# Graph layer with edge softmax: the sums of the weights in wider matmuls as a step of their own, and a new order of steps and gathers

## Chip, cores and metric

The kernel runs on one core of a Trainium2 chip. Its time is the device time of one execution in microseconds (us); lower is better. Before the change the median of 14 runs is 2747.45 us (2735.13 to 2751.48). Engine names: PE is TensorE (PEld its loading of weights), DVE is VectorE, ACT is ScalarE, POOL is GpSimd, SP is SyncE, which here issues the DMAs of loads and stores.

## The reference

There are 6250 nodes with 512 features and 100000 edges, sorted by destination. Two residual layers follow each other. The first one is graph attention with 8 heads of 64 features, the second one averages over neighbours.

```python
h = jnp.maximum(_layernorm(x), 0.0)
# first layer
h = leaky_relu(h @ W.T + b, 0.2).reshape(N, 8, 64)
e_src = sum(h * w_att_src, -1); e_dst = sum(h * w_att_dst, -1)
e = leaky_relu(e_src[src] + e_dst[dst], 0.2)
ex = exp(e - segment_max(e, dst)[dst])
s = segment_sum(ex, dst)
a = ex / s[dst] * edge_attr
x = x + segment_sum(h[src] * a[:, :, None], dst).reshape(N, 512)
# second layer: layernorm and relu again, then mean over the incoming
# edges, two matmuls, bias, layernorm with gamma and beta, residual
```

## The kernel before

**Stages.** A prologue computes `h` and the two attention terms and writes them to DRAM as a table with rows of 520 numbers (512 features and 8 source terms). Then comes the first edge layer, which is where the change lies; by the trace it runs from about 296 to 1440 us. The second edge layer and a tail end the program.

**Tiling of the first edge layer.** The edges, sorted by destination, are cut into four streams q = 0 to 3, worked side by side, as two pairs p = 0, 1 of two streams q2 = 0, 1 each. A window k (NW = 66 of them) takes T = 3 tiles j of 128 edges from each stream; the last window has one tile. The edges of a window of one stream fall on at most 64 destination nodes, so a one-hot matrix of 128 edges by 64 nodes (`oh`) adds a tile up by a matmul. The two streams of a pair fill the two halves of the 128 output partitions. Whatever belongs to a node that goes on in the next window is carried over by one more matmul with a selection matrix.

**Steps of a window.** A hand-written list, ORDER, is walked once per round k from -4 to 66. Each name in it is a step; STEPS gives it an offset, so that a round works on several windows at once (software pipelining). The instructions go to the engines' queues in this order, and each engine runs its own queue in order. The steps that the text speaks of, with line and engine:

- FT0, FT1 (L781, PE) transpose the one-hot matrices of a later window; FT0c, FT1c (L785, ACT) copy them out; FD (L793, PE) fetches destination terms; ECa, ECb (L810, ACT) pick the source terms out of the gathered rows; SSa, SSb (L802, PE) add them, transposed; EZ (L816, ACT) copies the logits.
- SCF (L822), NX (L829), SCR (L836), on DVE, are scans that find each segment's maximum; TE and TM (L848, PE) transpose logits and maxima back; CM (L853, ACT) copies them; LM (L860, DVE) is the leaky relu, SUB (L864, DVE) subtracts the maximum, EXP (L870, ACT) is the exponential `ex`, and AA (L878, L882, DVE) multiplies it by the edge attribute to the weight `aa`.
- D0a, D0b (p = 0, j = 0 and 1) and D1a, D1b (p = 1) multiply gathered rows by their weights on DVE (L942, both streams at once). The third tile is shared: D0c (L949, DVE) takes half of a stream, H01 to H03 and H10 to H13 (L961, ACT, four instructions each) take the rest.
- Apj (add_up, PE) adds tile j of pair p. L974 holds two matmuls (one for each stream) of 64 columns of weights and 512 moving columns. L977 holds two more with the same weights and 9 moving columns of `ex` (8 heads and a column of ones): the sums of the weights. C0, C1 (finish, PE) add the carry, L985 for the features and L986 for the sums. EV0, EV1 (evac, ACT) copy the results out of PSUM, L995 for the features and L997 for the sums; EV1 also issues the stores of the window. A float32 matmul leaves two matmul records and two weight-load records in the trace.
- OH (L762) and CS (L773), on DVE, build the one-hot and the carry selection. AT0, AT1 turn the edge attributes every tenth window. FL, FDf, FX, RS, RH, PF, F9a, F9b and RESC (offset windows below KR = 9 only) handle corrections of the first windows.
- S is a place for one step of "slot" work (L1042 to L1064: final division, residual, layernorm and relu of a finished block of 128 nodes, mostly on DVE), L the last of it. 48 of the 66 rounds have a slot.

**Gathers.** POOL issues one indirect DMA for each stream and tile (L719), twelve in a window, at the end of each round for the window four ahead (NB = 4 buffers). TILES gives their order, as pairs of stream q and tile j. A gather overwrites the rows of the window that has just been worked on, so the one for (q, j) waits for the add-up of tile j of pair q // 2.

**SP** issues, at the head of a round, the loads of edge data and slots, then the stores after EV1, then the store of the slot's relu.

Of the kernel before, what the change touches and what calls it, by code (L numbers as in the profile page):

```python
# [11 lines left out]
AF = mybir.ActivationFunctionType  # L12
# [3 lines left out]
N, D, E, H = 6250, 512, 100000, 8  # L16
# [20 lines left out]
AW = 521  # L37
# [7 lines left out]
def gnn_kernel(ctx, tc, x, srcp, dstp, attrp, wt0, b0, wsrc, wdst, wts, wtn, bias1, gamma1, beta1, out):  # L45
    nc = tc.nc
    V, A, G, S, P = nc.vector, nc.scalar, nc.gpsimd, nc.sync, nc.tensor
# [17 lines left out]
    def bank(tag, bufs=1):  # L65
        if tag == "m":
            m_[0] ^= 1
            tag, bufs = ("b", "f")[m_[0]], 1
        return ps.tile([128, 512], FT, name="ps_" + tag, tag=tag, bufs=bufs)
# [630 lines left out]
    GT, ES_, OHs, OHTs, PEN, AT, ZP, E_, PB, ET, MF, MR, NX, EX, AA, WS, WC, CS, FP, FD, RS, F9, SA, AP_ = ({} for _ in range(24))  # L700
    breg = {}

    def njof(k):
        return T if k < NW - 1 else 1
# [227 lines left out]
    BK, SV, A2 = {}, {}, {}  # L932
# [30 lines left out]
    def add_up(k, p, j):  # L963
        if j >= njof(k):
            return
        oh, ex, g_ = OHs[k], EX[k], GT[k]
        if j == 0:
            BK[p] = bank("w", 2)
            if p == 0:
                SV[k] = bank("sf"[k % 2])[:, 0:32].rearrange("p (a c) -> p a c", a=2)[:, :, 0:H + 1]  # L970
        w, sv = BK[p], SV[k]
        for q2 in range(2):
            r = slice(64 * q2, 64 * q2 + 64)
            P.matmul(w[r, :], oh[:, p, j, q2], g_[:, 2 * p + q2, j, 0:D], start=(j == 0), stop=False, skip_group_check=True)  # L974
        for q2 in range(2):
            r = slice(64 * q2, 64 * q2 + 64)
            P.matmul(sv[r, p], oh[:, p, j, q2], ex[:, j, 2 * p + q2], start=(j == 0 and p == 0), stop=False,  # L977
                     skip_group_check=True)

    def finish(k, p):  # L980

        w, sv = BK.pop(p), SV[k]
        if k:
            c = WC[k] if k < KR else WS[k - 1]
            P.matmul(w, CS[k][:, p], c[:, p, 0:D], start=False, stop=True, skip_group_check=True)  # L985
            P.matmul(sv[:, p], CS[k][:, p], c[:, p, D:AW], start=False, stop=True, skip_group_check=True)  # L986
        BK[k, p] = w
        if p:
            GT.pop(k)

    def evac(k, p):
        w, sv = BK.pop((k, p)), SV[k]
        if p == 0:
            WS[k] = lp.tile([128, 2, AW], FT, name="ws")
        A.activation(WS[k][:, p, 0:D], w, AF.Copy)  # L995
        if p:
            A.activation(WS[k][:, :, D:AW], sv, AF.Copy)  # L997
            for d_ in (OHs, EX, AA, A2, SV, WC, CS):
                d_.pop(k, None)
            WS.pop(k - 2, None)  # L1000
# [71 lines left out]


    TILES = [(int(t[0]), int(t[1])) for t in """
    10 00 11 20 01 21 31 32 30 12 22 02
    """.split()]

    for q in range(NQ):
# [8 lines left out]
    def later(f, end=NW):  # L1087

        return lambda k, *a: f(k, *a) if 0 < k < end else None

    def evac1(k):
        evac(k, 1)
        for p in range(2):
            store(k, p, acc0_d, AW)

    def evac0(k):
        evac(k, 0)
# [3 lines left out]
    def slot(w):  # L1101
# [8 lines left out]
        FT0=(4, front_turn, 0), FT0c=(4, front_copy, 0), FT1=(3, front_turn, 1), FT1c=(3, front_copy, 1),  # L1110
        FD=(3, front_dst), ECa=(3, soft_pick, 0), SSa=(3, soft_src, 0), ECb=(2, soft_pick, 1), SSb=(2, soft_src, 1), EZ=(2, soft_copy), SCF=(2, max_before), NX=(2, max_ahead),
        SCR=(1, max_all), TE=(1, soft_turn, 0), TM=(1, soft_turn, 1), CM=(1, soft_back), LM=(1, leaky),
        SUB=(1, soft_sub), EXP=(1, soft_exp), AA=(1, weigh),
        FL=(1, later(fac_leaky, KR)), FDf=(1, later(fac_sub, KR)), FX=(1, later(fac_exp, KR)), RS=(1, later(fac_rows, KR)),
        RH=(1, later(fac_diag, KR)), PF=(1, later(fac_spread, KR)), F9a=(1, later(fac_rest, KR)), F9b=(1, later(fac_all, KR)),
        RESC=(0, later(rescale, KR)), D0c=(0, message_part), D0a=(0, message, 0, 0), D0b=(0, message, 0, 1), D1a=(0, message, 1, 0),
        D1b=(0, message, 1, 1),
        A00=(0, add_up, 0, 0), A01=(0, add_up, 0, 1), A02=(0, add_up, 0, 2),
        A10=(0, add_up, 1, 0), A11=(0, add_up, 1, 1), A12=(0, add_up, 1, 2), C0=(0, finish, 0), C1=(0, finish, 1),
        EV0=(0, evac0), EV1=(-1, evac1), OH=(4, onehot), CS=(0, later(carry_sel)))  # L1120
    STEPS.update({f"H{p}{i}": (0, message_act, p, i) for p in range(2) for i in range(4) if p or i})
    ORDER = """
    FT1 D1a S S S D0a S D0b H10 A00 CS H11 TE H02 EV1 NX S H01 SCR S D0c A01 RESC TM H03 ECb AT0 FL FT1c SSb OH A10 A02
    S FDf D1b H12 FX RH L CM LM EZ H13 SUB C0 EXP AT0c RS AT1 PF SCF A11 AT1c FT0 S S S F9a A12 FD F9b ECa S SSa S EV0
    FT0c AA S C1
    """.split()

    def late_x(i):
# [6 lines left out]
    for k in range(-4, NW + 1):  # L1135
        sl_ = slot_run(slot(k - 3)) if slot(k - 3) is not None and slot(k - 3) not in LATE else none()
        c, kk = divmod(k, CH)
# [54 lines left out]
    def late_stats(i):  # L1192
        s6 = lp.tile([128, 6], FT, name="s6_0")
        V.bn_stats(s6, keep[:, i])
        V.bn_aggr(lmv[:, i], s6)

    def late_scales(i):
        c, mv = late_part(i), lmv[:, i[0]:i[-1] + 1]
        yield from rstd_of(lp, mv[:, :, 1], LATES, "lt", c[:, :, 9], n=len(i))
        V.scalar_tensor_tensor(c[:, :, 10], mv[:, :, 0], -1.0, c[:, :, 9], op0=OP.mult, op1=OP.mult)  # L1200
# [22 lines left out]
    a = late_scales(one)  # L1223
# [277 lines left out]
    def late_newton(i):  # L1501
        if not 0 <= i < NLATE:
            return
        v = LT[i]
        for _ in v["gen"]:
            yield True
        nb = small.tile([128, 1], FT, name="nb1")
        V.scalar_tensor_tensor(nb, v["mv"][:, 0:1], -1.0, v["rs"], op0=OP.mult, op1=OP.mult)
        v["nb"] = nb
        yield True  # L1510
# [74 lines left out]
    k = NW - 1  # L1585
# [28 lines left out]
    for i in range(-1, NLATE + 4):  # L1614
# [13 lines left out]
        a, b = late_stats(i - 1), late_newton(i - 3)  # L1628
# [9 lines left out]
    with tc.If(fv > 0):  # L1638
# [32 lines left out]
        def logit(ix):  # L1671
            hg = lp.tile([128, RW], FT, name="ghg")
            fetch(hg, h0_d, ix[:, 0:1])
            e = lp.tile([128, H], FT, name="ge")
            fetch(e, ed_d, ix[:, 1:2])
            V.tensor_tensor(out=e, in0=e, in1=hg[:, D:RW], op=OP.add)
            V.scalar_tensor_tensor(e, e, 0.2, e, op0=OP.mult, op1=OP.max)
            return hg, e
# [13 lines left out]
        with tc.For_i(0, NE * 128, 128) as r:  # L1692
            ix, eq = ends(r)
            hg, e = logit(ix)
# [13 lines left out]
        with tc.For_i(0, NE * 128, 128) as r:  # L1708
            ix, eq = ends(r)
            hg, e = logit(ix)  # L1710
# [64 lines left out]
```

## Time and profile before

The profiled execution took 2745.76 us; its span is 2744.0 us, 1.76 us lie around it. It is 1.69 us below the median of the 14 runs.

| stretch, us | length | PE busy | DVE busy | ACT busy | POOL busy | granted PE clock |
|---|---|---|---|---|---|---|
| 0 to 296, prologue | 296 | 213.13 | 214.18 | 138.72 | 174.69 | 0.94, then 0.84 |
| 296 to 440, first edge layer, start | 144 | 116.86 | 90.46 | 77.15 | 85.07 | 0.84 |
| 440 to 1440, first edge layer | 1000 | 825.70 | 676.33 | 594.78 | 637.46 | 0.89 |
| 1440 to 1480, between the layers | 40 | 34.76 | 33.82 | 21.98 | 7.53 | 0.91 |
| 1480 to 2700, second edge layer | 1220 | 985.55 | 559.66 | 267.96 | 793.82 | 0.89 |
| 2700 to 2744, tail | 44 | 20.60 | 30.71 | 11.74 | 17.87 | 0.81 |

| group of instructions, whole span | records | busy us | mean ns |
|---|---|---|---|
| L719 POOL, gathers of the first edge layer | 784 | 765.1 | 976 |
| L974 PE, features added up | 1568 | 503.0 | 699 |
| L961 ACT, steps H | 1788 | 452.0 | 338 |
| L942 DVE, steps D | 260 | 311.5 | 1210 |
| L985 PE, carry of the features | 228 | 143.6 | 709 |
| L977 weight loads | 776 + 792 | 69.1 + 67.4 | 156, 149 |

How to read such lines: a group's line has line number, engine, operation, output and inputs, shapes, count, then busy time and mean duration, and behind the bar the engine's idle time just before these instructions, with what ended it. On a timeline the first number is the start, the second the duration; idle time before the instruction stands in brackets. The ends of matmuls are modelled, so durations of neighbours on PE overlap; the text takes differences between starts. "issue" is a wait for which the profile shows no releaser.

### The profile page before, as it was taken

The numbers are of one execution on the slowest core, as the hardware profiler recorded it, in microseconds if no ns is written. First come the engines' busy times: TensorE is split into PE (matmuls) and PEld (weight loads), VectorE is DVE, ScalarE is ACT, GpSimd is POOL, SyncE is SP. The second block draws the span as 40 slices with busy tenths as digits, with TensorE's granted clock in tenths as the row PEclk, the third lists the DMA queues.
The fourth block names the chain that finished last, engine by engine and source line by source line (L and its number), as shares of the span: only waits on it lengthen the run. The fifth ranks groups of instructions, "written<-read, shape, count | busy, mean of one in ns | idle before, by whom it ended". The sixth has DMA issues, their size and how long they took to land.

```text
span 2744.0 us, 35822 instructions
## 1 busy us (share of the span) xinstructions
PE 2196.6 (80%) x9688; PEld 1090.0 (40%) x9688; DVE 1605.2 (58%) x3323; ACT 1112.3 (41%) x3439; POOL 1716.4 (63%) x1679
## 2 busy tenths in 40 slices
PE   7994488878788888788884488898887879888875
PEld 5762244433333433343432133343443434343433
DVE  8876466566767667676766222354544545454556
ACT  5751355565565656565654111122222222222212
POOL 4665566666666666666652666666666666666662
PEclk9996689899989898888887689898999989998988
DMA  6634576777777878888874767787878777777862
GB/s 204 203 114 134 153 210 195 224 242 231 239 236 240 250 233 242 243 242 240 239 232 140 242 212 237 230 253 249 257 247 263 242 247 246 252 252 249 256 206 90
DMA packets 264718, 611.73 MB, mean 223 GB/s; under 512 B 63604, under 2 KB 74372, under 8 KB 264510
## 3 DMA queue, kind: packets, MB, share of 16 engines
q0 software_dynamic: 125440, 414.35, 50.7%
q1 hardware_dynamic: 138494, 193.97, 21.6%
q8 instruction: 79, 1.29, 0.2%
q14 instruction: 129, 1.06, 0.1%
q10 hardware_dynamic: 576, 1.05, 0.1%
HBM read 511.44 MB, written 97.76 MB: 222 GB/s over the span
## 4 chain that ended last, share of the span: by engine, by line
PE 49%; issue 17%; DVE 12%; POOL 8%; DMA 6%; ACT 4%; another core or an unknown queue 2%; SPq 2%; ACTq 0%; DVEq 0%; POOLq 0%
PE ps_w L974 12%; PE ps_w L1285 7%; POOL g L1249 6%; PE ps_w L985 4%; PE ps_b L573 4%; PE ps_s L1285 3%; PE ps_f L573 3%; PE ps_z L793 3%; DMA gbuf<-h_d,idx 2%; DMA g<-h_d,idx 2%; PE ps_t L781 2%; POOL gbuf L719 2%; PE ps_z L802 1%; DVE gbuf L942 1%
## 5 line engine op out<-in xcount | busy, mean ns | idle before, releaser
L719 POOL DMA_INDIRECT gbuf<-h_d,idx x784 | 765.1, 976 | 439.7 <-issue 188.3
L1249 POOL DMA_INDIRECT g<-h_d,idx x784 | 773.7, 987 | 386.7 <-issue 218.2
L974 PE MATMUL ps_w<-gbuf,oh 128*64 128x512 f32 x1568 | 503.0, 699 | 31.1 <-issue 21.2
L961 ACT ACTIVATE gbuf<-gbuf,aa 128x64 f32<-128x64 f32 x1788 | 452.0, 338 | 2.2 <-DVE aa L882 1.7
L1285 PE MATMUL ps_w<-g,oh 128*64 128x512 f32 x1048 | 332.1, 662 | 108.6 <-issue 56.7
L942 DVE TENSOR_TENSOR gbuf<-gbuf,ps_c 128x1024 f32<-128x1024 f32 x260 | 311.5, 1210 | 0.0
L1285 PE MATMUL ps_s<-g,oh 128*64 128x512 f32 x520 | 159.1, 647 | 31.6 <-issue 29.1
L1285 PEld LDWEIGHTS ps_w<-g,oh 128*64 128x64 f32 x1048 | 75.6, 144 | 258.1 <-issue 241.9
L860 DVE SCALAR_TENSOR_TENSOR et<-ps_b,et 128x192 f32<-128x192 f32 x66 | 23.4, 355 | 259.0 <-issue 203.7
L608 POOL TENSOR_TENSOR pr<-hr,watt 128x1024 f32<-128x1024 f32 x47 | 113.5, 2416 | 90.9 <-DVE hr L606 75.1
L995 ACT ACTIVATE ws<-ps_w 128x512 f32<-128x512 f32 x132 | 78.4, 594 | 198.8 <-PE ps_t L781 32.7
L985 PE MATMUL ps_w<-ws,cs 128*128 128x512 f32 x228 | 143.6, 709 | 11.1 <-issue 10.2
L1367 DVE TENSOR_TENSOR lo<-ps_z,hi 128x512 fp32r<-128x512 f32 x48 | 33.1, 689 | 202.7 <-issue 162.5
L1311 DVE CAST chi<-ws 128x512 fp32r<-128x512 f32 x130 | 56.9, 437 | 161.0 <-issue 87.0
L977 PEld LDWEIGHTS ps_f<-ex,oh 128*64 128x64 f32 x776 | 69.1, 156 | 169.1 <-issue 168.5
L977 PEld LDWEIGHTS ps_s<-ex,oh 128*64 128x64 f32 x792 | 67.4, 149 | 164.8 <-issue 164.5
L1366 ACT ACTIVATE hi<-ps_z 128x512 fp32r<-128x512 f32 x48 | 28.7, 598 | 255.4 <-remote 101.0
L974 PEld LDWEIGHTS ps_w<-gbuf,oh 128*64 128x64 f32 x1568 | 93.2, 149 | 93.7 <-issue 72.0
L802 PE MATMUL ps_z<-ident,es 128*32 128x128 f32 x392 | 72.3, 297 | 65.1 <-DVE nx L829 21.3
L762 DVE TENSOR_TENSOR oh<-ps_c,dsr 128x768 f32<-128x768 f32 x130 | 122.6, 944 | 0.1
L1367 DVE TENSOR_TENSOR lo<-ps_t,hi 128x512 fp32r<-128x512 f32 x55 | 37.7, 685 | 139.5 <-ACT hi L1366 85.1
L793 PE MATMUL ps_z<-oht,edb 128*32 128x384 f32 (+1 forms) x264 | 109.4, 539 | 12.4 <-issue 11.0
(395 smaller groups left out, 4123.6 us busy)
## 6 DMA issues: line engine op xcount, KB each, us to landing
sx<-x SPq DMA_DIRECT2D x95, 256.0 KB
acc_d<-ws SPq DMA_DIRECT2D x182, 130.2 KB
acc_d<-ws SPq DMA_DIRECT2D x182, 128.0 KB
h_d<-hr SPq DMA_DIRECT2D x49, 260.0 KB
gbuf<-h_d,idx POOLq DMA_INDIRECT x784
g<-h_d,idx POOLq DMA_INDIRECT x784
sa<-acc_d SPq DMA_DIRECT2D x48, 260.5 KB
s<-acc_d SPq DMA_DIRECT2D x48, 256.0 KB
```

Source lines behind the costliest of these rows:

```text
L573: P.matmul(pt, a_[:, k], w_[:, k], start=not last[0], stop=stop and k == 3 and w_ is whi_ and a_ is lo)
L608: (G if t < NT - 2 else V).tensor_tensor(out=pr, in0=hr[:, None, 0:D].to_broadcast([128, 2, D]), in1=watt, op=OP.mult)
L719: G.indirect_dma_start(out=g_[:, q, j, :], out_offset=None, in_=h0_d, in_offset=bass.IndirectOffsetOnAxis(ap=idx[:, q, c:c + 1], axis=0))
L762: V.tensor_tensor(out=oh.rearrange("p a j b n -> p (a j b) n"), in0=c_iota[:, None, :].to_broadcast([128, 4 * T, M]), in1=dsr[:, k].rearra ...
L793: P.matmul(z[0:NQ * H, 0:n], ed_tile(k, p), oht[:, p, 0:n], start=(p == 0), stop=False, skip_group_check=True)
L942: eng.tensor_tensor(out=x4, in0=x4, in1=(AA if eng is V else A2)[k][:, i, q].unsqueeze(3).to_broadcast([128, 2, H, D // H]), op=OP.mult)
L961: A.activation(x_, x_, AF.Copy, scale=A2[k][:, T - 1, 2 * p + q2, h:h + 1])
L974: P.matmul(w[r, :], oh[:, p, j, q2], g_[:, 2 * p + q2, j, 0:D], start=(j == 0), stop=False, skip_group_check=True)
L977: P.matmul(sv[r, p], oh[:, p, j, q2], ex[:, j, 2 * p + q2], start=(j == 0 and p == 0), stop=False, skip_group_check=True)
L985: P.matmul(w, CS[k][:, p], c[:, p, 0:D], start=False, stop=True, skip_group_check=True)
L1249: G.indirect_dma_start(out=g_[:, q2, j, :], out_offset=None, in_=h1_d[0:NT * 128, :], in_offset=bass.IndirectOffsetOnAxis(ap=idx[:, 2 * p ...
L1285: P.matmul(BK[p][64 * q2:64 * q2 + 64, :], OHs[k][:, p, j, q2], GT[k, p][:, q2, j, :], start=(j == 0), stop=False, skip_group_check=True)
```

## The change

1. Add-up loses its two small matmuls. A new step SV (add_ones) makes all the sums of the weights of a window: for each pair and tile one matmul whose weights are the one-hots of both streams side by side (128 columns) and whose moving operand is `ex` of both streams (18 columns). The output has 128 partitions by 18 columns for a pair; only the 9 columns that belong to a partition's own stream are used.
2. The carry of the sums (L986) gets its 9 columns twice, so that it fits the wider output. Copying the sums out (L997) becomes two instructions of 64 partitions each.
3. The gathers' order TILES is another.
4. ORDER is another: 72 names where there were 71 (the new one is SV), 13 of them S as before. Tables, offsets and buffers stay.

```diff
     def add_up(k, p, j):
...
-            if p == 0:
-                SV[k] = bank("sf"[k % 2])[:, 0:32].rearrange("p (a c) -> p a c", a=2)[:, :, 0:H + 1]
-        w, sv = BK[p], SV[k]
+        w = BK[p]
         for q2 in range(2):
             r = slice(64 * q2, 64 * q2 + 64)
             P.matmul(w[r, :], oh[:, p, j, q2], g_[:, 2 * p + q2, j, 0:D], start=(j == 0), stop=False, skip_group_check=True)
-        for q2 in range(2):
-            r = slice(64 * q2, 64 * q2 + 64)
-            P.matmul(sv[r, p], oh[:, p, j, q2], ex[:, j, 2 * p + q2], start=(j == 0 and p == 0), stop=False,
-                     skip_group_check=True)
+
+    def add_ones(k):
+
+        oh, ex = OHs[k], EX[k]
+        SV[k] = sv = bank("sf"[k % 2])[:, 0:64].rearrange("p (a b c) -> p a b c", a=2, b=2)[:, :, :, 0:H + 1]
+        for p in range(2):
+            for j in range(njof(k)):
+                P.matmul(sv[:, p], oh[:, p, j].rearrange("e b n -> e (b n)"), ex[:, j, 2 * p:2 * p + 2], start=(j == 0 and p == 0),
+                         stop=False, skip_group_check=True)
...
-            P.matmul(sv[:, p], CS[k][:, p], c[:, p, D:AW], start=False, stop=True, skip_group_check=True)
+            P.matmul(sv[:, p], CS[k][:, p], c[:, p, None, D:AW].to_broadcast([128, 2, H + 1]), start=False, stop=True, skip_group_check=True)
...
-            A.activation(WS[k][:, :, D:AW], sv, AF.Copy)
+            for q2 in range(2):
+                r = slice(64 * q2, 64 * q2 + 64)
+                A.activation(WS[k][r, :, D:AW], sv[r, :, q2], AF.Copy)
...
-    10 00 11 20 01 21 31 32 30 12 22 02
+    10 01 11 00 20 30 21 22 31 12 02 32
...
+        SV=(0, add_ones), A00=(0, add_up, 0, 0), A01=(0, add_up, 0, 1), A02=(0, add_up, 0, 2),
...
-    FT1 D1a S S S D0a S D0b H10 A00 CS H11 TE H02 EV1 NX S H01 SCR S D0c A01 RESC TM H03 ECb AT0 FL FT1c SSb OH A10 A02
-    S FDf D1b H12 FX RH L CM LM EZ H13 SUB C0 EXP AT0c RS AT1 PF SCF A11 AT1c FT0 S S S F9a A12 FD F9b ECa S SSa S EV0
-    FT0c AA S C1
+    S H01 D0a D1a D0c H02 S NX TE FT1 ECb D0b EV1 H11 A00 S SCR SV H12 H03 A01 RESC FL L FT1c S AT0 S TM A10 S FDf OH
+    CM FX RH CS S LM A02 AT0c SUB AT1 RS SSb C0 S PF ECa S H13 EZ EXP D1b S A11 H10 AT1c FT0 S FT0c S F9a F9b SCF AA
+    EV0 A12 FD SSa C1 S
```

More of the change, by code (lines that the diff above doesn't have):

```diff
@@ L965, in add_up @@
             return
-        oh, ex, g_ = OHs[k], EX[k], GT[k]
+        oh, g_ = OHs[k], GT[k]
         if j == 0:
             BK[p] = bank("w", 2)
-            if p == 0:
-                SV[k] = bank("sf"[k % 2])[:, 0:32].rearrange("p (a c) -> p a c", a=2)[:, :, 0:H + 1]
-        w, sv = BK[p], SV[k]
+        w = BK[p]
         for q2 in range(2):
@@ L1117, in gnn_kernel @@
         D1b=(0, message, 1, 1),
-        A00=(0, add_up, 0, 0), A01=(0, add_up, 0, 1), A02=(0, add_up, 0, 2),
+        SV=(0, add_ones), A00=(0, add_up, 0, 0), A01=(0, add_up, 0, 1), A02=(0, add_up, 0, 2),
         A10=(0, add_up, 1, 0), A11=(0, add_up, 1, 1), A12=(0, add_up, 1, 2), C0=(0, finish, 0), C1=(0, finish, 1),
```

## The prediction

> **What bounds the kernel now.** All times are us. I read the page's head first, then the busy times of the stretch 440 to 1440, in which the first edge layer turns at a steady rate, then the groups of that stretch, and last the timelines of VectorE (DVE), ScalarE (ACT) and TensorE (PE) through one window.
>
> ```profile
> span 2744.0 us, 35822 instructions
> ...
> PE 2196.6 (80%) x9688; PEld 1090.0 (40%) x9688; DVE 1605.2 (58%) x3323; ACT 1112.3 (41%) x3439; POOL 1716.4 (63%) x1679
> ```
>
> ```profile
> 440.00:1440.00 1000.00, 825.70 (x4351) 394.88 (x4349) 676.33 (x1350) 594.78 (x2233) 637.46 (x656) 0.89 0.79 237
> ```
>
> ```profile
> L719 POOL DMA_INDIRECT gbuf<-h_d,idx x656 | 637.5, 972 | 357.3 <-issue 155.4 <-remote 75.6 <-PE ps_w L974 36.4
> ...
> L977 PE MATMUL ps_f<-ex,oh 128*64 128x9 f32 x672 | 51.7, 197 | 29.6 <-issue 27.3 <-DMA penb<-pen_d 1.8
> ...
> L977 PE MATMUL ps_s<-ex,oh 128*64 128x9 f32 x652 | 48.8, 195 | 31.5 <-issue 31.4
> ...
> L860 DVE SCALAR_TENSOR_TENSOR et<-ps_b,et 128x192 f32<-128x192 f32 x55 | 19.7, 358 | 238.1 <-issue 186.4 <-ACT et L853 48.3 <-ACT gbuf L961 3.4
> ```
>
> L860 (step LM) runs once a window: 55 times in 1000, a **period of 18.18**. No engine is full: PE 826 and DVE 676 of 1000, at a mean granted clock of 0.89. DVE has one long wait, ahead of LM: 238.1/55 = 4.33 a window. LM waits for CM (ACT, L853), which waits for TM (PE, L848), which waits for SCR (DVE, L836), which stands behind all of DVE's work since the last LM. So the period is a loop through three engines, LM to SCR to TM to CM to LM, with DVE idle in its second part. One turn on the timelines, DVE first:
>
> ```profile
> 869.83 0.36 DVE L860 SCALAR_TENSOR_TENSOR et<-ps_b,et 128x192 f32<-128x192 f32 x1 [5.89 <-issue]
> ...
> 879.67 0.99 DVE L836 TENSOR_TENSOR_SCAN mr<-penb,nx,mf 32x384 f32<-32x384 f32 x1
> ...
> 880.66 0.38 DVE L949 TENSOR_TENSOR gbuf<-gbuf,ps_c 128x256 f32<-128x256 f32 x1
> ...
> 887.74 0.36 DVE L860 SCALAR_TENSOR_TENSOR et<-ps_b,et 128x192 f32<-128x192 f32 x1 [4.65 <-issue]
> ```
>
> ```profile
> 887.38 0.33 ACT L853 ACTIVATE et<-ps_b 128x192 f32<-128x192 f32 x1 [5.06 <-remote]
> ```
>
> ```profile
> 877.39 0.28 PE L986 MATMUL ps_s<-ws,cs 128*128 128x9 f32 x2
> 877.53 0.53 PE L781 MATMUL ps_t<-ident,oh 128*128 128x128 f32 x3
> ...
> 878.90 0.24 PE L977 MATMUL ps_f<-ex,oh 128*64 128x9 f32 x4
> 879.07 0.37 PE L848 MATMUL ps_b<-ident,e 32*128 32x32 f32 x3
> ...
> 880.71 0.37 PE L848 MATMUL ps_b<-ident,mr 32*128 32x32 f32 x3 [0.20 <-issue]
> ...
> 883.23 0.23 PE L977 MATMUL ps_f<-ex,oh 128*64 128x9 f32 x2
> 884.21 0.17 PE L977 MATMUL ps_f<-ex,oh 128*64 128x9 f32 x1 [0.75 <-issue]
> 885.77 0.17 PE L977 MATMUL ps_f<-ex,oh 128*64 128x9 f32 x1 [1.38 <-issue]
> 886.48 1.73 PE L985 MATMUL ps_w<-ws,cs 128*128 128x512 f32 x2 [0.54 <-issue]
> ...
> 888.37 1.98 PE L974 MATMUL ps_w<-gbuf,oh 128*64 128x512 f32 x4
> ```
>
> LM to the end of SCR took 880.66 - 869.83 = 10.83; TM left at once (880.71) and ended at 881.08; yet CM started only at 887.38, 6.30 later (median of the layer 5.7, from its trace). In that gap PE crawls: the last four L977 records of A02 run from 883.23 to 886.48, against 0.17 for four elsewhere (878.90 to 879.07). Why CM's release comes so late no view says. PE also matters ahead of TM: in 20 of 49 windows TM left over 0.4 after SCR's end, because A00, TE and A01 before it were late. From LM's start, A11 starts at a median of 0.98 (mean 1.05), and TM on average at 12.11; from A11's start to A01's end PE needs a median of 9.86, a mean of 10.65.
>
> **The change part by part.** There are 65 full windows; the last has one tile, and is left out.
>
> *Small matmuls.* An add-up loses its two, four records: 0.17 each time, six add-ups: -1.02. SV adds six with 128 columns of weights. The trace has no such matmul with 18 moving columns; the nearest row is L986 (128 columns, 9 moving), 0.28/2 = 0.14 by starts (877.39 to 877.53): +0.84. Bounds: 0.085 each, the price of today's 64-column ones (+0.51), and 0.38, if none of the weight loads is hidden (two of about 0.19 by the L986 load rows; +2.28). I take 0.84, net -0.18, of which TM's side gets +0.16 (SV, less A11, A12, A00, A01) and the stretch behind TM -0.34 (A10, A02).
>
> The trace's median weight load is 137 ns for L977 (64 columns) and 190 ns for L986 (128). The Trainium skill, page "TensorE: Matmul & The Clock Gate", section "LDWEIGHTS (loading the stationary operand)", lets a load cost its columns over 1.2 ns, which speaks against the change: an estimate of 24 loads of 53 ns against 12 of 107 ns, 1.28 either way and nothing won. By that rule this term is near 0, by the rows -0.18.
>
> *Stops.* L977's records of 440 to 1440 have 29.6 + 31.5 = 61.1 of idle time ahead of them, 1.11 a window. Counted by step (gaps over 0.2), 70 stops make 61.0 of it: A02 44 (37.6), A12 16 (18.1), A11 7, A10 3; A00 and A01, where SV will stand, none. Either the stops belong to these matmuls (then up to -1.11) or to the stretch, and the next instruction takes them (0). Half of the records go; I take half, -0.55.
>
> *DVE's leg, LM to SCR.* Into it come D1b (1.13 by starts) and D0c (0.30, 880.66 to 880.96); out go CS (0.34) and two steps of the slot work, L1045 and L1056 (0.60 each); a 0.25 wait ahead of L175 goes too, as L175 comes later. 10.83 + 1.43 - 1.79 = 10.47, in the 48 windows that carry slot work; in the other 18, 7.40 + 1.09 = 8.49. Mean (48 x -0.36 + 18 x 1.09)/66 = +0.04. Between SCR and LM, D1b leaves and the slot steps and CS enter, about 3.0 against 2.5; the 4.33 wait hides that. Without the wait it costs 0.5.
>
> *A11 behind D1b.* D1b moves behind SUB, and A11 (window's second tile of pair 1) needs it. D1b ends at least 0.39 + 0.18 + 1.2 = 1.8 after LM's start, so A11 can no longer start at 0.98: +0.8, and all behind it on PE waits (FT0, A12, FD, SSa, C1, TE, FT1, A00, SV, A01, TM). Where SCR is last, this is hidden; where PE is last, 20 of 49 windows, it counts: 0.41 x 0.8 = +0.33. H10 behind EXP (H 4 x 0.338, ACT) ends some 2.5 after LM; A12 starts after A11 and FT0, 1.5 later than A11, and is just covered; if not, up to 1 more.
>
> *At nothing.* The second 64-partition ACT copy in evac (L997, 0.18; ACT is 59% busy). The 18-column carry operand (L986, inside the 0.14). Shape changes on PE go from 12 to 14 a window; the rows show no gap at one beyond the prices above. SSb goes behind A02, ahead of C0: NX, its reader, comes a DVE round later. The SP queue's instructions keep their order (loads at the head of the round, stores after EV1, h store with the last slot step). The gathers: twelve at 1.25 from issue to issue are 15.0 of 18.18, so POOL has 3.2 spare. The second gather now waits for A01 rather than A00 (1.5 later on PE); the spare hides it, and without it a window would be up to 1.5 longer.
>
> **Sum.** -0.18 - 0.55 + 0.04 + 0.33 = -0.36 a window, x 65 = -23.4. The profiled execution took 2745.76 (span 2744.0 and 1.76 around it): 2722.4; the median of the runs is 1.69 above that execution: **2724**. With the stops gone entirely (-0.92 a window) 2688, with none gone (+0.19) 2760. About 5 us (0.2%) is what a measurement here can tell from no change.
>
> **Rivals.**
>
> *PE's leg decides in every window (slower).* The place is A11 behind D1b, the price the +0.8 above; it decides once PE's leg, A11's start plus 10.65 + 0.16, lies behind SCR's end in all windows and not in 20 of 49. 1.85 + 10.81 = 12.66 against today's 12.11 for LM to TM: +0.55, and no stop goes, since they move to the next instruction. x 65 = +36: 2783. If the stops fall on SV as well, some 0.35 a window more, 2805. For it: SCR's mean end is only 11.46 after LM, so PE at 12.66 would pass it. Against it: 10.65 holds stops of A12 and late D0a's that may shrink.
>
> *Nothing moves.* The stretch between TM and CM has its own length, whatever PE issues in it, and the other terms cancel: -0.18 to +0.04 a window is 2737 to 2750. For it: no view names what releases CM. Against it: four terms must meet near zero.
>
> *The late release goes.* It comes while PE works through A10 and A02; without their small matmuls it could come when TM ends. The next floor is POOL's 15.0: 3.2 x 65 = 208, 2540; half of it, 2640. For it: 61 us of stops on just the instructions that go. Against it: the gap begins ahead of the first stop.
>
> **How the numbers follow.** Forecast 0.38, PE's leg 0.38, nothing moves 0.10, the release goes 0.14. Faster by over 0.2%: 0.36 (forecast) + 0.14 = 0.50; within: 0.02 + 0.08 = 0.10; slower: 0.38 + 0.02 (of nothing moves) = 0.40. Forecast and slower rival are level, so the forecast's own range, 2688 to 2760, stands beside the wide one: 2640 (half of the late release) to 2805 (PE's leg with stops), which leaves 2 in 10 out.
>
> **What would show it.** Right: L860's idle below 4.3 a window, few stops left on the new small matmul's rows, TM to CM below 5.7, a period near 17.8. SV at 0.14 each by starts shows that price. Wrong to the slow side: A11's L974 records waiting for DVE, L848 (TM) held by PE and not by SCR, a period near 18.7. Wrong to the fast side: CM straight behind TM and POOL's idle time gone. If the stops sit as before but on C0, SSb or A11, they belong to the stretch, and the -0.55 falls.

## The result and the profile after

The changed kernel takes 2759.77 us (median of 10 runs, 2756.41 to 2769.58) beside 2746.14 for the kernel before (48 runs): a ratio of 1.0055, interval 1.0044 to 1.0066. It is slower by 13.6 us, where 23 us faster was forecast. The range (2640 to 2805) holds it, the direction was wrong. The five jobs of the experiments below found the kernel before at different times (2747.57, 2393.03, 2392.55, 2778.50, 2746.76), so every ratio is to the kernel before of the same job.

The profiled execution of the changed kernel took 2773.64, which is 13.9 above its median; against the 2745.76 of before, its 27.9 more are about twice the typical difference. Of these, 22.8 lie between the first LM and the last (1180.4 against 1157.6). The counts from its trace have to be read with that in mind.

First the page's head, the busy times of the stretch 440 to 1440, and the groups of that stretch, all of the changed kernel (L972 is the old L974, L980 is SV):

```profile
span 2771.8 us, 34424 instructions
...
PE 2230.3 (80%) x8904; PEld 1058.3 (38%) x8904; DVE 1598.4 (58%) x3323; ACT 1134.8 (41%) x3505; POOL 1716.4 (62%) x1679
```

```profile
440.00:1440.00 1000.00, 838.96 (x3618) 359.05 (x3615) 655.79 (x1318) 601.55 (x2245) 632.17 (x649) 0.89 0.78 232
```

```profile
L719 POOL DMA_INDIRECT gbuf<-h_d,idx x649 | 632.6, 975 | 366.9 <-issue 159.0 <-PE ps_w L972 56.1 <-PE ps_z L802 40.2
L972 PE MATMUL ps_w<-gbuf,oh 128*64 128x512 f32 x1296 | 404.1, 697 | 150.2 <-DVE gbuf L942 71.9 <-ACT gbuf L961 46.1 <-issue 28.6
...
L980 PE MATMUL ps_f<-ex,oh 128*128 128x18 f32 x324 | 41.8, 269 | 0.0
L980 PE MATMUL ps_s<-ex,oh 128*128 128x18 f32 x324 | 41.0, 266 | 0.1
...
L829 DVE TENSOR_TENSOR_SCAN nx<-penb,ms,ps_z 32x256 f32<-32x256 f32 x54 | 39.6, 733 | 142.7 <-PE ps_z L802 43.5 <-remote 26.4 <-PE ps_z L793 19.6
...
L816 ACT ACTIVATE e<-ps_z 32x384 f32<-32x384 f32 x54 | 25.3, 469 | 59.5 <-remote 53.2 <-PE ps_t L781 3.9 <-issue 1.5
L860 DVE SCALAR_TENSOR_TENSOR et<-ps_b,et 128x192 f32<-128x192 f32 x54 | 19.2, 356 | 127.5 <-issue 95.0 <-ACT et L853 21.4 <-ACT oht L785 6.3
```

Most of what the forecast wanted to see is there, and it did not help. The 648 small records of this stretch have no stop ahead of them any more (0.0 and 0.1, where the old ones had 29.6 and 31.5). LM waits 127.5/54 = 2.36 a window, against 4.33, and the gap from TM's end to CM's start is 2.9, against 5.4. But the idle time came back elsewhere: NX waits 2.64 a window (0.64 before, from its row), SCF 0.94 (0.08), EZ on ACT 59.5/54 = 1.10 (0.12). Over 50 windows DVE and ACT are idle at the same time for 199 us; before it was 166. Before, 130 of it ended with CM; now 61 ends with CM, 63 with NX, 40 with EZ and 27 with FT0c.

The period's median even fell (17.92 against 18.04), while its mean rose (18.50 against 18.21). The loss sits in single windows. In 9 of 49, EZ starts over 3 us after LM, which is called late from here on (its median is 1.45; before, none was late). One of them, on ACT:

```profile
1025.61 0.32 ACT L853 ACTIVATE et<-ps_b 128x192 f32<-128x192 f32 x1
...
1026.46 1.05 ACT L961 ACTIVATE gbuf<-gbuf,aa 128x64 f32<-128x64 f32 x4
1034.23 0.48 ACT L816 ACTIVATE e<-ps_z 32x384 f32<-32x384 f32 x1 [6.72 <-remote]
1034.62 0.27 ACT L870 ACTIVATE ex<-et 128x96 f32<-128x96 f32 x1
1034.79 1.05 ACT L961 ACTIVATE gbuf<-gbuf,aa 128x64 f32<-128x64 f32 x4
```

and the same time on PE:

```profile
1026.80 0.41 PE L802 MATMUL ps_z<-ident,es 128*32 128x128 f32 x2
...
1028.32 1.08 PE L972 MATMUL ps_w<-gbuf,oh 128*64 128x512 f32 x4
1029.33 0.55 PE L781 MATMUL ps_t<-ident,oh 128*128 128x128 f32 x3
1035.89 1.98 PE L972 MATMUL ps_w<-gbuf,oh 128*64 128x512 f32 x4 [6.01 <-ACT gbuf L961]
```

SSb (L802) ends at 1027.21 by the profile, EZ gets its result at 1034.23. That is the late release which the prediction saw behind TM, now on another step. And here it has followers: on ACT, EXP stands behind EZ and H10 behind EXP; on PE, A12 (1035.89) waits for H10, and FD and SSa stand behind A12; on DVE, SCF waits too, AA behind it, and NX later for FD and SSa:

```profile
1034.74 1.00 DVE L822 TENSOR_TENSOR_SCAN mf<-penb,mf,ps_z 32x384 f32<-32x384 f32 x1 [6.47 <-ACT e L816]
...
1041.45 0.73 DVE L829 TENSOR_TENSOR_SCAN nx<-penb,ms,ps_z 32x256 f32<-32x256 f32 x1 [2.59 <-PE ps_z L793]
```

Before, the same gap lay ahead of CM and LM, and one wait took it.

### The profile page after: what moved, and what is told of

Same layout as the page of the kernel before. It is cut to its first block, busy times and chain, and to the rows that moved or that the text cites. A ratio compares the mean times of both kernels' runs of the same rounds, so it can differ in the third digit from the quotient of the medians.

```text
span 2771.8 us, 34424 instructions
## 1 busy us (share of the span) xinstructions
PE 2230.3 (80%) x8904; PEld 1058.3 (38%) x8904; DVE 1598.4 (58%) x3323; ACT 1134.8 (41%) x3505; POOL 1716.4 (62%) x1679
## 4 chain that ended last, share of the span: by engine, by line
PE 48%; issue 15%; DVE 12%; POOL 8%; another core or an unknown queue 5%; DMA 5%; ACT 5%; SPq 1%; ACTq 0%; POOLq 0%; DVEq 0%
PE ps_w L972 10%; PE ps_w L1290 8%; POOL g L1254 6%; PE ps_b L573 4%; PE ps_f L573 4%; PE ps_s L1290 4%; PE ps_z L793 3%; PE ps_w L988 3%; ACT gbuf L961 2%; DVE gbuf L942 2%; POOL gbuf L719 2%; PE ps_t L781 2%; PE ps_z L802 2%; PE ps_w L1297 2%
## 5 line engine op out<-in xcount | busy, mean ns | idle before, releaser
L972 PE MATMUL ps_w<-gbuf,oh 128*64 128x512 f32 x1568 | 486.6, 698 | 165.0 <-DVE gbuf L942 83.3
L1290 PE MATMUL ps_w<-g,oh 128*64 128x512 f32 x1048 | 337.8, 673 | 121.6 <-issue 114.0
L972 PEld LDWEIGHTS ps_w<-gbuf,oh 128*64 128x64 f32 x1568 | 95.4, 149 | 258.2 <-issue 107.7
L785 ACT ACTIVATE oht<-ps_t 128x384 f32<-128x384 f32 x132 | 64.1, 486 | 257.3 <-PE ps_z L793 43.5
L829 DVE TENSOR_TENSOR_SCAN nx<-penb,ms,ps_z 32x256 f32<-32x256 f32 x66 | 48.1, 728 | 199.4 <-remote 76.1
L793 PE MATMUL ps_z<-oht,edb 128*32 128x384 f32 (+1 forms) x264 | 120.9, 590 | 18.8 <-DVE mf L822 14.4
L988 PE MATMUL ps_w<-ws,cs 128*128 128x512 f32 x228 | 128.6, 646 | 0.1
L781 PE MATMUL ps_t<-ident,oh 128*128 128x128 f32 x392 | 81.7, 323 | 27.8 <-issue 26.5
L1371 ACT ACTIVATE hi<-ps_t 128x512 fp32r<-128x512 f32 x55 | 32.9, 598 | 172.6 <-remote 87.4
```

The source lines that it names most:

```text
L781: P.transpose(pt[:, j * 128:j * 128 + 128], OHs[k][:, p, j].rearrange("e b n -> e (b n)"), ident)
L793: P.matmul(z[0:NQ * H, 0:n], ed_tile(k, p), oht[:, p, 0:n], start=(p == 0), stop=False, skip_group_check=True)
L1290: P.matmul(BK[p][64 * q2:64 * q2 + 64, :], OHs[k][:, p, j, q2], GT[k, p][:, q2, j, :], start=(j == 0), stop=False, skip_group_check=True)
```

## The experiments

**First job** (before 2747.57): the two parts of the change apart, and two steps moved back. Theory 1: the late release falls on SSb's result. Theory 2: A11 and A12 wait for D1b and H10, which were moved. Theory 3: SV costs.

*e1_sv_only*: old ORDER and TILES, SV behind A00.

```diff
-    FT1 D1a S S S D0a S D0b H10 A00 CS H11 TE H02 EV1 NX S H01 SCR S D0c A01 RESC TM H03 ECb AT0 FL FT1c SSb OH A10 A02
+    FT1 D1a S S S D0a S D0b H10 A00 SV CS H11 TE H02 EV1 NX S H01 SCR S D0c A01 RESC TM H03 ECb AT0 FL FT1c SSb OH A10 A02
```

> The old order of steps and of gathers, with only the sums as a step of their own, put right behind A00. Theory 1 (the loss comes from the order: a gap of some 4 us in each window, in which PE's results are released late, falls on SSb/EZ or NX in some windows): no loss here, 2735 to 2750, since SSb and NX stand where they stood. Theory 2 (the order's loss is that A11 and A12 wait for D1b and H10): the same. Theory 3 (SV itself costs: its twelve records take 1.44 us by starts in the trace of the changed kernel, against 1.02 for what it replaces, all of it ahead of TM): +0.42 x 65 = 27 us, about 2773.

2753.11, ratio 1.0022 (1.0010 to 1.0033): +5.5 us, 3 above the range of theories 1 and 2 and 20 below theory 3. Its groups, 440 to 1440:

```profile
L972 PE MATMUL ps_w<-gbuf,oh 128*64 128x512 f32 x1320 | 444.0, 706 | 50.9 <-issue 40.1 <-DVE gbuf L942 5.5 <-ACT gbuf L961 3.3
...
L829 DVE TENSOR_TENSOR_SCAN nx<-penb,ms,ps_z 32x256 f32<-32x256 f32 x55 | 40.0, 727 | 31.3 <-PE ps_w L972 16.5 <-remote 8.0 <-PE ps_b L848 3.5
...
L816 ACT ACTIVATE e<-ps_z 32x384 f32<-32x384 f32 x55 | 25.6, 465 | 9.1 <-PE ps_w L972 6.1 <-remote 2.5 <-DVE et L860 0.4
...
L860 DVE SCALAR_TENSOR_TENSOR et<-ps_b,et 128x192 f32<-128x192 f32 x55 | 19.7, 358 | 252.4 <-issue 187.6 <-ACT et L853 62.4 <-ACT sx L1069 2.4
```

With the small matmuls gone from A02 and A10, LM waits 4.59 a window, not less than before, and the gap from TM to CM is 5.60 (before 5.40). PE's stops now stand ahead of L972 (50.9, before 26.8) and FT's L781 (24.0, before 5.0). So they belong to the stretch, not to the small matmuls. SV's price, by starts, is 1.44 a window (median, in this kernel and in the changed one).

*e2_order_only*: new ORDER without SV, new TILES, sums in the add-ups as before. The edit to the kernel before, with ORDER's other two lines as in the change:

```diff
-    10 00 11 20 01 21 31 32 30 12 22 02
+    10 01 11 00 20 30 21 22 31 12 02 32
...
-    FT1 D1a S S S D0a S D0b H10 A00 CS H11 TE H02 EV1 NX S H01 SCR S D0c A01 RESC TM H03 ECb AT0 FL FT1c SSb OH A10 A02
+    S H01 D0a D1a D0c H02 S NX TE FT1 ECb D0b EV1 H11 A00 S SCR H12 H03 A01 RESC FL L FT1c S AT0 S TM A10 S FDf OH
...
```

> The new order of steps and gathers, with the sums of the weights left in the add-ups as before. Theory 1 and theory 2: slower than before by as much as the whole change or more, 2755 to 2775. Theory 3: no slower than before, 2735 to 2748.

2848.01, ratio 1.0377 (1.0355 to 1.0399): the order alone costs 100 us, and SV in that order is worth about 87 of them. Theories 1 and 2 had the direction, but no theory had it so dear. Its rows, 440 to 1440:

```profile
L829 DVE TENSOR_TENSOR_SCAN nx<-penb,ms,ps_z 32x256 f32<-32x256 f32 x50 | 36.7, 734 | 112.3 <-PE ps_z L802 69.5 <-PE ps_z L793 26.9 <-remote 10.2
...
L816 ACT ACTIVATE e<-ps_z 32x384 f32<-32x384 f32 x50 | 23.9, 478 | 223.3 <-remote 199.1 <-PE ps_t L781 15.6 <-issue 4.1
...
L860 DVE SCALAR_TENSOR_TENSOR et<-ps_b,et 128x192 f32<-128x192 f32 x50 | 17.6, 353 | 44.5 <-issue 41.0 <-ACT sx L1064 2.2 <-ACT gbuf L961 1.2
```

EZ waits 4.47 a window and is late in 44 of 49; LM's wait has shrunk to 0.89. Most of the late release has moved from CM to EZ, and with it there the period is 1.8 a window longer (20.02).

*e3_ssb_back*: the changed kernel with SSb ahead of A10 again.

```diff
-    S H01 D0a D1a D0c H02 S NX TE FT1 ECb D0b EV1 H11 A00 S SCR SV H12 H03 A01 RESC FL L FT1c S AT0 S TM A10 S FDf OH
-    CM FX RH CS S LM A02 AT0c SUB AT1 RS SSb C0 S PF ECa S H13 EZ EXP D1b S A11 H10 AT1c FT0 S FT0c S F9a F9b SCF AA
+    S H01 D0a D1a D0c H02 S NX TE FT1 ECb D0b EV1 H11 A00 S SCR SV H12 H03 A01 RESC FL L FT1c S AT0 S TM SSb A10 S FDf OH
+    CM FX RH CS S LM A02 AT0c SUB AT1 RS C0 S PF ECa S H13 EZ EXP D1b S A11 H10 AT1c FT0 S FT0c S F9a F9b SCF AA
```

> The changed kernel with one step moved back: SSb stands again ahead of A10, right behind TM, and not behind A02. Theory 1: the windows in which EZ starts over 3 us after LM (9 of 50 in the changed kernel) go, the period's mean comes near its median of 17.9 and the time to 2740 to 2752. Theory 2 and theory 3: no difference to the changed kernel, 2755 to 2765.

2750.69, ratio 1.0016 (0.9999 to 1.0033), where the changed kernel has 1.0055. Its rows:

```profile
L829 DVE TENSOR_TENSOR_SCAN nx<-penb,ms,ps_z 32x256 f32<-32x256 f32 x55 | 40.4, 734 | 158.4 <-PE ps_z L802 46.9 <-remote 43.4 <-PE ps_t L781 29.1
...
L816 ACT ACTIVATE e<-ps_z 32x384 f32<-32x384 f32 x55 | 25.5, 463 | 0.1
...
L860 DVE SCALAR_TENSOR_TENSOR et<-ps_b,et 128x192 f32<-128x192 f32 x55 | 19.6, 357 | 154.2 <-issue 131.5 <-ACT et L853 19.2 <-ACT oht L785 2.0
```

EZ no longer waits (0.1) and is late in no window; the period's mean is 18.16. Theory 1 expected 2740 to 2752, and it came; theories 2 and 3 expected 2755 to 2765. What is left of the loss is no more than SV alone costs (1.0022).

*e4_d1b_h10_back*: the changed kernel with D1b behind OH (ahead of LM) and H10 behind H03.

```diff
-    S H01 D0a D1a D0c H02 S NX TE FT1 ECb D0b EV1 H11 A00 S SCR SV H12 H03 A01 RESC FL L FT1c S AT0 S TM A10 S FDf OH
-    CM FX RH CS S LM A02 AT0c SUB AT1 RS SSb C0 S PF ECa S H13 EZ EXP D1b S A11 H10 AT1c FT0 S FT0c S F9a F9b SCF AA
+    S H01 D0a D1a D0c H02 S NX TE FT1 ECb D0b EV1 H11 A00 S SCR SV H12 H03 H10 A01 RESC FL L FT1c S AT0 S TM A10 S FDf OH D1b
+    CM FX RH CS S LM A02 AT0c SUB AT1 RS SSb C0 S PF ECa S H13 EZ EXP S A11 AT1c FT0 S FT0c S F9a F9b SCF AA
```

> The changed kernel with two steps moved back: D1b ahead of LM (behind OH) and H10 ahead of A01's neighbour H11's successors (behind H03). Theory 2: A11 no longer waits for DVE (71.9 us of idle time in the changed kernel) nor A12 for ACT (46.1), the loop gets 0.8 us a window shorter where PE is last, 2735 to 2748. Theory 1: A12 and SSa come earlier, but EZ can still be late, and D1b in the idle time before LM costs nothing: part of the loss stays, 2745 to 2757. Theory 3: 2755 to 2765.

2774.54, ratio 1.0095 (1.0074 to 1.0116): slower still, above what any theory expected (2765 at most). The moved steps did what they should:

```profile
L972 PE MATMUL ps_w<-gbuf,oh 128*64 128x512 f32 x1280 | 398.3, 690 | 39.6 <-DVE gbuf L942 31.9 <-issue 7.2 <-ACT gbuf L961 0.3
...
L822 DVE TENSOR_TENSOR_SCAN mf<-penb,mf,ps_z 32x384 f32<-32x384 f32 x54 | 54.0, 1001 | 117.8 <-issue 72.5 <-ACT e L816 36.6 <-ACT gbuf L961 8.8
...
L816 ACT ACTIVATE e<-ps_z 32x384 f32<-32x384 f32 x54 | 25.4, 470 | 75.5 <-remote 42.2 <-PE ps_w L972 27.0 <-PE ps_t L781 4.3
```

The add-ups' waits fell from 150.2 to 39.6, yet EZ is late in 14 windows in place of 9, and SCF (L822) waits 117.8 in place of 50.7. Theory 2 falls as the account of the loss: taking those waits away gained nothing. What they cost by themselves is not shown, as the two steps, where they now stand, can cost something too.

**Second job** (before 2393.03) and **third** (2392.55).

*f1_tiles_old*: the changed kernel with the old TILES.

```diff
-    10 01 11 00 20 30 21 22 31 12 02 32
+    10 00 11 20 01 21 31 32 30 12 22 02
```

*f2_sv_late*, and again *g2_sv_late*: e1 with SV behind A02.

```diff
-    FT1 D1a S S S D0a S D0b H10 A00 SV CS H11 TE H02 EV1 NX S H01 SCR S D0c A01 RESC TM H03 ECb AT0 FL FT1c SSb OH A10 A02
+    FT1 D1a S S S D0a S D0b H10 A00 CS H11 TE H02 EV1 NX S H01 SCR S D0c A01 RESC TM H03 ECb AT0 FL FT1c SSb OH A10 A02 SV
```

> The changed kernel with the gathers in the old order; steps and SV stay changed. If the gathers' order matters for where the late release falls: 2770 or more (worse, as the steps' order was made with the other one) or below 2752 (better). If it costs nothing, as the prediction has it: 2755 to 2765, as the changed kernel.

> The old order with SV, but SV stands behind A02 (behind TM, in the stretch in which DVE and ACT wait) and not behind A00. If PE's leg ahead of TM sets the period, TM leaves 0.4 to 1.5 us earlier after SCR in the windows where PE is last, and the time falls by 0.4 x 1.4 x 65 = 36 us against SV behind A00 (2753): about 2717. If the end of the late release is set by something else, which TM does not move, the gap behind TM only grows: 2744 to 2755.

> The old order with SV behind A02, in the stretch where DVE and ACT wait. On a chip with 2747 before: 2744 to 2755 if the end of the gap is not TM's to move; about 2717 if PE's leg ahead of TM sets the period. On a chip with 2393 before: 0.3% slower, as measured there.

f1 1.0048 (1.0032 to 1.0064); f2 1.0031 (1.0022 to 1.0041) and 1.0027 (1.0014 to 1.0041). What the expectations asked could not be read: in these jobs the long gap is not there (TM to CM 2.7 in f2, 0.3 in f1, 1.9 in f3 below), and EZ has no wait in f1 (0.03 a window). So the 0.48% that f1 loses there is no late release; SV alone (f2) loses 0.31%, and what makes the rest is not shown. The period of f2 is 15.23. The row of the gathers in 440 to 1240, in f2 and then, for comparison, in the kernel before as profiled for the prediction:

```profile
L719 POOL DMA_INDIRECT gbuf<-h_d,idx x632 | 608.7, 963 | 192.5 <-issue 121.2 <-DMA gbuf<-h_d,idx 21.0 <-PE ps_w L972 10.7
```

```profile
L719 POOL DMA_INDIRECT gbuf<-h_d,idx x527 | 511.5, 971 | 288.4 <-issue 124.9 <-remote 61.6 <-PE ps_w L974 32.9
```

One gather takes the same (963 and 971 ns), but in 800 us there are 632 and not 527. POOL's time beyond 1.25 from issue to issue is 0.21 a window in f2 and 3.22 in the kernel before. Whether the gathers' order mattered stays open, as the changed kernel did not run in that job.

*f3_half_rows*, again as *g3_half_rows* and, in the fourth job, *h3_half_rows*: the kernel before with gathers of half the bytes.

```diff
+            half = NB <= k < NW - 3
-            G.indirect_dma_start(out=g_[:, q, j, :], out_offset=None, in_=h0_d,
+            G.indirect_dma_start(out=g_[:, q, j, 0:RW // 2] if half else g_[:, q, j, :], out_offset=None,
+                                 in_=h0_d.rearrange("n (a b) -> (n a) b", a=2) if half else h0_d,
```

> The kernel before, with each of its gathers of the first edge layer from window 4 to 62 reading rows of 260 numbers and not of 520: as many gathers, packets, steps and waits, half the bytes; it works on wrong rows. If the late release comes from the gathers' traffic, the gap between TM and CM shrinks from 5.4 to 2 us or less and the period from 18.2 to near POOL's 15.0: 2540 to 2600. If it comes from PE's own work or from the chain of waits, the period stays above 17.5 and the time above 2700.

> The kernel before with rows of 260 numbers in its gathers of windows 4 to 62 (half the bytes, wrong rows), once more, wanted on a chip on which the kernel before takes 2747: on one where it takes 2393 the bytes changed nothing (0.09%), since its period of 15.2 there is POOL's twelve issues of 1.25. If the late release comes from the gathers' traffic, the gap behind TM shrinks from 5.4 to 2 us or less and the time to 2540 to 2600; if not, above 2700. On a chip with 2393 before: no change again.

> The kernel before with half the bytes in its gathers of windows 4 to 62 (wrong rows). Where before takes about 2747: 2540 to 2600 if the late release comes from the gathers' traffic, above 2700 if not. Where it takes 2393: no change, as measured twice.

1.0009 (0.9998 to 1.0020), 1.0004 (0.9993 to 1.0016), and in the fourth job, where the kernel before takes 2778.50, 0.9992 (0.9978 to 1.0005). There the gap from TM to CM is 5.21 at half the bytes. The core moved 147 GB/s in 440 to 1240 in place of 236:

```profile
440.00:1240.00 800.00, 648.56 (x3441) 309.66 (x3440) 532.69 (x1056) 467.82 (x1761) 505.00 (x523) 0.89 0.54 147
```

The bytes do not make the gap.

*f4_sv_twice*, *g4_sv_twice* and, in the fifth job, *i2_sv_twice*: e1 with SV's matmuls done twice, in add_ones.

```diff
-        SV[k] = sv = bank("sf"[k % 2])[:, 0:64].rearrange("p (a b c) -> p a b c", a=2, b=2)[:, :, :, 0:H + 1]
+        bk = bank("sf"[k % 2])
+        SV[k] = sv = bk[:, 0:64].rearrange("p (a b c) -> p a b c", a=2, b=2)[:, :, :, 0:H + 1]
...
+        dup = bk[:, 64:128].rearrange("p (a b c) -> p a b c", a=2, b=2)[:, :, :, 0:H + 1]
+        for p in range(2):
+            for j in range(njof(k)):
+                P.matmul(dup[:, p], oh[:, p, j].rearrange("e b n -> e (b n)"), ex[:, j, 2 * p:2 * p + 2], start=False,
+                         stop=False, skip_group_check=True)
```

> The old order with SV behind A00, where SV does its matmuls twice (the second time into columns that nobody reads): 1.44 us more of PE a window, ahead of A01 and TM. If PE's time or its leg to TM sets the period: +0.5 to +1.4 a window, 2785 to 2845. If the end of the gap is set by something that PE does not move: TM comes 1.4 later, the gap behind it gets 1.4 shorter, 2750 to 2765.

> The old order with SV behind A00, its matmuls done twice (1.44 us more of PE a window, into columns that nobody reads). On a chip with 2393 before this cost 2.2%: PE was busy all the time. On one with 2747 before: if the end of the gap behind TM is set by something that PE does not move, TM comes later and the gap gets shorter, 2750 to 2770; if PE's time counts there too, +0.8 a window or more, 2800 and above.

> The old order, SV behind A00 with its matmuls done twice (1.44 us more of PE a window). Where before takes 2393 it was 2.0 and 2.2% slower. Where before takes 2747 or more: if the end of the gap behind TM is not PE's to move, the added time comes out of the gap, at most 0.7% slower; if PE's time counts in full there too, 65 x 1.44 = 94 us, 3.4% slower.

1.0224 (1.0202 to 1.0246) and 1.0202 (1.0180 to 1.0225) without the gap; in the fifth job, with it, 1.0138 (1.0115 to 1.0160). There 1.44 us more of PE a window ahead of TM made TM later by 2.6 (14.55 after LM, in e1 11.92), and the gap behind TM shorter by 2.3 (3.29, in e1 5.60); the period grew by 0.60 (18.85 against 18.25). The gap is elastic: most of what PE adds ahead of TM comes out of it. The measured 1.4% lies between the two cases of the expectation (at most 0.7%, or 3.4%), so neither holds as it stands.

*g1_nx_behind_d0b*, again as *i3_nx_behind_d0b*: e3 with D0b ahead of NX.

```diff
-    S H01 D0a D1a D0c H02 S NX TE FT1 ECb D0b EV1 H11 A00 S SCR SV H12 H03 A01 RESC FL L FT1c S AT0 S TM SSb A10 S FDf OH
+    S H01 D0a D1a D0c H02 S D0b NX TE FT1 ECb EV1 H11 A00 S SCR SV H12 H03 A01 RESC FL L FT1c S AT0 S TM SSb A10 S FDf OH
```

> The changed kernel with SSb ahead of A10 again, and D0b ahead of NX in place of behind it, so that DVE works while NX waits for SSa. In the kernel with SSb moved alone, NX waited 1.8 us behind SSa's end on average but in 6 of 50 windows started over 12 us after LM, with DVE and ACT idle for 34 us. If those waits are the rest of the loss: 1.13 us saved in each late window and some 0.3 in the others, 2725 to 2745 where before takes 2747. If the late release only moves to CM: 2745 to 2755, no gain.

> The changed kernel with SSb ahead of A10 and D0b ahead of NX. Where before takes 2393 it was 0.24% slower than before. Where before takes 2747 or more: if the waits of NX are the rest of the loss (SSb moved alone was at 1.0016), 0.99 to 1.000; if the late release only moves on, 1.001 to 1.004.

1.0024 (1.0010 to 1.0037) without the gap, and 1.0003 (0.9992 to 1.0014) with it, in the fifth job. With the two steps moved, the changed kernel is level with the one before. The step from e3's 1.0016 to 1.0003 lies within the intervals, and 1.0003 lies between the two cases of the expectation, so whether NX's waits were the rest of the loss stays open.

**Fourth job** (before 2778.50): *h1_change* is the changed kernel, *h2_order_only* the order alone.

> The changed kernel itself, beside the kernel before on the chip that this job gets. Where before takes about 2393 (no late release seen in three kernels there, POOL's issues 1.25 apart without a stop): if the late release on SSb and EZ was the loss, it is absent, and what remains is SV's price and A11 behind D1b against POOL's floor of 15.0: 0.0 to 0.5% slower. Where before takes about 2747: 0.55% slower, as measured.

> The new order with the sums left in the add-ups. Where before takes about 2747 it was 3.8% slower, with EZ late in 45 of 50 windows. Where before takes about 2393: if the loss was the late release on EZ, at most 1% slower; if it was the order itself (PE's leg, DVE's waits), again 3 to 4%.

1.0039 (1.0021 to 1.0057) and 1.0363 (1.0338 to 1.0389): the two losses are there again, with EZ late in 6 and in 46 of 49 windows.

**Fifth job** (before 2746.76). *i1_few_gathers*: the kernel before with nine gathers a window in place of twelve.

```diff
+            if NB <= k < NW - 3 and j == 2 and q:
+                continue
```

> The kernel before without the gathers of the third tile of streams 1 to 3 in windows 4 to 62: nine gathers a window and not twelve, the rest unchanged (the left-out rows keep older data). Where before takes about 2393, if POOL's twelve issues of 1.25 set the period there, POOL's floor falls to 11.3 and the time by up to 59 x 3 = 177 us, until PE or the loop binds. Where before takes 2747 or more: if the late release comes from POOL's gathers, the gap behind TM shrinks and the time falls by 60 us or more; if not, it stays within 1%.

2532.01, ratio 0.9211 (0.9190 to 0.9232): 215 us less, 3.6 for each of 59 windows, nearly the 3 x 1.25 of the issues left out. The rows of gathers (now L721) and LM (now L862), 440 to 1240:

```profile
L721 POOL DMA_INDIRECT gbuf<-h_d,idx x487 | 479.1, 984 | 304.0 <-issue 105.7 <-PE ps_w L976 87.6 <-PE ps_b L850 37.7
...
L862 DVE SCALAR_TENSOR_TENSOR et<-ps_b,et 128x192 f32<-128x192 f32 x55 | 19.6, 357 | 51.6 <-ACT sx L1066 18.3 <-ACT et L855 18.2 <-issue 9.8
```

The period is 14.65, and LM waits 51.6/55 = 0.94 a window. POOL's time beyond 1.25 per issue is still 3.31 a window, as with twelve (3.22). The gap from TM to CM went from 5.40 to 2.21. So the loop through LM and TM had slack of some 3 us: with fewer gathers, what the round gets shorter comes out of the gap. The run leaves out a quarter of the gathers' packets and bytes along with the issues; *h3_half_rows* clears the bytes, and no run parts packets from issues.

## Why the prediction was wrong, point by point

**The bound.** "The period is a loop through three engines, LM to SCR to TM to CM to LM" failed. Leaving out three gathers moved the period by 3.6 a window, doubling SV on that loop by 0.6 for 1.44. The round follows the number of gathers: POOL's twelve issues of 1.25 and its stops, 3.2 a window together, make it up. I had read POOL's 3.2 as spare. But these stops are not POOL's own either. Two of its gathers in the window of the prediction, where CM starts at 887.38:

```profile
884.43 0.95 POOL L719 DMA_INDIRECT gbuf<-h_d,idx  x1 [0.30 <-issue]
887.53 0.95 POOL L719 DMA_INDIRECT gbuf<-h_d,idx  x1 [2.15 <-remote]
```

Of the semaphore that PE's finished work counts up, the trace records no step between 879.91 and 887.18, and then six by 887.44; CM and this gather of POOL both start right behind the first of them. Of POOL's 112 stops over 0.5 us in 440 to 1440 (191 us), the profile puts 72 (115 us) down to PE. So POOL waits for PE's late results, and yet with fewer gathers these come sooner. Which of the two begins it is not shown.

**SSb at nothing: the step that turned the sign.** I covered SSb behind A02 with "NX, its reader, comes a DVE round later". But NX reads only the first two tiles, which SSa made; the readers of SSb are EZ and SCF, and EZ stands ahead of EXP on ACT. Moved there, SSb's result is caught by the late release, and EXP, H10, A12, SSa and NX follow. Moving it back took the ratio from 1.0055 to 1.0016; in the order without SV, EZ late in 44 of 49 windows goes with a loss of 3.8%.

**Stops, -0.55.** The rows lost their idle time exactly (61.1 to 0.1), and the time did not: e1 shows the stops on other matmuls and LM's wait at 4.59. My own sentence, "or to the stretch, and the next instruction takes them (0)", was the right end; I took the middle between the two for no measured reason. With no stop gone the prediction's sum gives 2760, which is the measured time, but by luck: that sum has SV at -0.18 and SSb at nothing.

**SV, +0.84.** Measured 1.44, 0.24 a matmul where L986 gave 0.14, inside the bounds of 0.51 to 2.28. The net on PE is +0.42 and not -0.18; in e1 only 0.08 a window of it (5.5 us) reaches the time. The weight loads are 195 and 191 ns for 128 columns, 154 and 151 for 64: they grew by 1.3. By the rule in the Trainium skill, page "TensorE: Matmul & The Clock Gate", section "LDWEIGHTS (loading the stationary operand)", load time goes with the columns; the estimate worked out from it is that half as many loads of twice the width win nothing. The measured loads grew less than that, but the step was dearer still, so the estimate (no gain) was nearer than my row.

**DVE's leg, +0.04.** LM to SCR's end has a median of 12.44, before 11.14. What the count left out is that NX now waits in this leg, 2.64 a window in place of 0.64, for SSa, which stands behind A12.

**A11 behind D1b, +0.33.** The size was right: A11 starts 1.91 after LM (median), before 0.98, and 1.8 was the least predicted. What it cost is not shown: e4 took most of the wait away and was slower.

**The rivals.** "PE's leg decides" had the sign; its place, A11, is not borne out, as e4 took that wait away and gained nothing. "Nothing moves" was right that the gap does not come from what PE issues in it (e1: 5.60 without the small matmuls). The gap has no length of its own, though (2.21 in i1, 3.29 in i2), and it can move to a worse step. Order and SV also don't add: SV alone +5.5, order alone +100, both +13.6. Why the small matmuls make the order so much worse is not shown; with them, SSb stands behind 8 more matmul records (those of A10 and A02) in the stretch where the releases are late.

## What to carry to other kernels

When a wait has no releaser that explains it, don't price it as work on the path: make one engine's round shorter or longer on purpose, and see whether the wait gives way. Before moving a step into such a stretch, follow every reader of its result, and what stands behind that reader on its own queue: a late result costs little where one idle engine waits for it, and much where a whole chain is queued behind it.

## What the runs showed of the hardware

A matmul's end in the trace can lie long before its reader is let go: 7.0 us from SSb's modelled end to EZ's start in the window above, with PE itself standing idle for the last 4.4 of them (1029.88 to 1034.23). From TM's modelled end to CM's start it was 5.40 on average in the kernel before. The granted clock does not explain it: from 881.08 to 887.38, the gap shown in the prediction, it was 1.00, and 24 of the 45 gaps over 3 us in that trace lie wholly at 1.0. The Trainium skill, page "Perfetto Trace Analysis", section "Tensor Engine Instruction (MATMUL, LD_WEIGHTS)", says that TensorE's end times are estimated and not observed, and that the semaphore is updated only once PSUM has acknowledged the writes; the trace agrees that the shown end is not the release, and no run here shows what the 7.0 us are.

The same program took 13 to 14% less time in two jobs (2393 against 2747 to 2778), with the same length of gathers on POOL (963 and 971 ns), a mean granted clock of 0.95 (f2's profile) against 0.88, and without POOL's stops of 3.2 us a window. The jobs with 2393.03 and with 2778.50 ran on chips of the same number (9). What makes the stops in the other jobs is open: they are there with half the bytes, with nine gathers, in either order and with SV once or twice (3.1 to 5.2 us a window).
